# Global attention of a sandwich layer: the lead of the row maxima, its side work, and which engine splits the local weights

## The chip, the cores and the metric

The kernel runs on one core of a Trainium2 chip. The metric is the device time of one launch in microseconds (us). The core has five engines that run side by side, each through its own instructions in order: TensorE (PE, with its weight loads PEld), VectorE (DVE), ScalarE (ACT), GpSimd (POOL) and SyncE (SP), which issues the DMAs. [...]

## The reference, cut to what matters

Two sequences of 2048 tokens with 256 channels go through two residual blocks. In the first, a layer norm is followed by a global attention with 16 heads of 16 channels, rotary positions and a softmax over all 2048 keys, then an output projection and a second layer norm:

```python
q = _rope(proj(Wq, bq)); k = _rope(proj(Wk, bk)); v = proj(Wv, bv)
scores = jnp.einsum('bhtd,bhsd->bhts', q, k) / scale
attn = jax.nn.softmax(scores, axis=-1)
out = jnp.einsum('bhts,bhsd->bhtd', attn, v)
...
x = x + _layernorm(_L0_attn_ref(_layernorm(x), ...))
x = x + _layernorm(_L0_ffn_ref(_layernorm(x), ...))
```

The second block is two layers of local attention (8 heads of 64 channels, windows of 128 tokens) with a gated feed-forward network each. The change touches the first block and the passage to the second.

## The kernel before, in words

**Units and steps.** The global attention is cut into 32 units: for each of two batches `b`, four groups `g` of four heads, and four blocks `k` of 512 queries. `attend` (L505) takes a unit in 16 steps, one for each 128 keys: per step four score matrices `se` of 128 keys by 512 queries on PE (L543), an exponential of each on ACT (L548, `pe<-se`), and the products with the values on PE (L517, `pv`, one step later). The first four units (`HALVED`) are done in two halves of eight steps.

**Maxima ahead.** The exponentials need the row maxima first. `row_max` (L437) computes the scores a second time with the queries as rows (`sm`, L412), and DVE reduces each 128 by 512 tile to one column (L452, `pm<-sm`). Four such reductions are one step's worth. When a unit (or half) is complete, `finish_max` (L469) combines the columns on DVE (`nm`, L472), splits the result in two parts on POOL (`mp`, L477 and L478; on DVE for the last unit), and yields. `DELAY` groups of four reductions later the rest follows: a transpose on PE (`tn`, L481), a copy on ACT (`mt`, L485), a DMA to a DRAM tile (`md`, L488) and four DMAs that put the maxima into two extra rows of the unit's queries `qs` (L491), so that the score product subtracts them. The last unit's rest is done by `last_steps` (L895) in its third step.

**The main loop** (L844) runs `len(units) * NT - TAIL` = 486 steps. In step n it draws in turn, so that the engines' orders are written out by hand: three pieces of `attend` and three of the maxima, interleaved; in every fourth step (`EVERY`) two more maxima as long as the lead is below `TAIL` (the maxima start 13 steps ahead and get half a step further each time, up to 26); one piece of the side work that multiplies on PE (`side.step(PRODUCTS)`); the rest of the step; then pieces on other engines of `early` and `side`. Within `with tc.manual_schedule(engines=ENGINES)`, PE, ACT, DVE and POOL take their instructions in the order of the program; SP's order is the framework's.

**Side work.** `early` normalizes the blocks of batch 1 on POOL and builds the rotary tables of the local layers there. `side` projects: queries of blocks 2 and 3 of batch 0 (`project_qk`, L314), then keys, values and queries of the four blocks of batch 1, and later the closing of finished blocks (`close_in_pieces`, L620). `project_qk` has twelve products, in each of two halves followed by a copy on ACT (`raw`, L329) and two multiplications on POOL (`rotation`, L333); at its end `to_dram_steps` adds six POOL instructions (L342 to L350) and two stores. `load_queries` (L398) reads a unit's queries back when `(n + lead + 3) // NT` reaches its number. In step 3, `output_weights` (L805) loads and splits the output projection's weights and computes its bias with two fp32 matmuls, all at once.

**The startup** ends at L768: `merged` takes pieces of several strands in the order of planned times (first blocks, keys, values, queries of blocks 0 and 1, the first maxima); the framework schedules them.

**The tail.** The last `TAIL` = 26 steps of `attend` have no maxima left beside them. They are a strand with a planned period `STEP` of 2.5 us, ending at `LAST` = 20, beside the strands of the local layers, whose first window starts at 0. Steps here work on double tiles: ACT takes 1024 columns at a time. The planned times of the closing of blocks (−46), of what is left of the side work (−50) and of the weights of the first local layer (`WEIGHTS_FROM` = −50) are set beside it. `load_attn_weights` (L957) copies four pieces of 1024 columns to `attnh` (L196) and subtracts them from the raw weights to `attnl` (L197), both on DVE, each placed behind the last reduction of the maxima (`tc.issue_after(reduced[-1])`).

Of the kernel before, what the change touches and what calls it, by code (L numbers as in the profile page):

```python
# [20 lines left out]
P = 128  # L21
# [26 lines left out]
def tile_sandwich(  # L48
# [152 lines left out]
    def in_order(strands):  # L201


        heap = [(t, n, t, g) for n, (t, g) in enumerate(strands)]
        heapq.heapify(heap)
        return heap
# [225 lines left out]
                yield 1.2 * n  # L432


    reduced, unfinished = [], []

    def row_max():  # L437

        due = []
        for u, (b, g, k) in enumerate(units):  # L440
            q, keys = qs[u], ks[g % 2]
            for span in spans(u):
                if (u, span) == (0, spans(0)[0]):
                    continue
                pm = small.tile([P, 4, 4, NBLK], F32, tag="pm", name="pm", bufs=2)
                for t in range(*span):

                    for j, half in [(j, half) for j in (0, 2) for half in (0, 2)]:
                        for kk, i in ((half, 1), (half, 0), (half + 1, 1), (half + 1, 0)):
                            sc = one("sm", "sm")  # L450
                            scores(q, keys, j + i, t, kk, sc)
                            ins = nc.vector.tensor_reduce(  # L452
                                pm[:, t, j + i, kk : kk + 1], sc, AX.X, ALU.max
                            )
                            reduced[:] = [ins.ins]
# [41 lines left out]
    o_raw = {}  # L497
    sums_d = {}

    TAIL, HALVED, DELAY = 26, 4, 4  # L500


    IN_TURN = {1: (0, 1, 2, 3), 2: (0, 2, 1, 3)}
# [196 lines left out]
    def first_block(k):  # L700
        xt = x0[k]
        for t in range(4):
            shift, rstd = stats0[k][t]
            nc.scalar.activation(xt[:, t, :], xt[:, t, :], AF.Identity, bias=shift, scale=rstd)
        tag = ("qs", "o4", "o4", "t4")[k]
        xh = t4("xh", F32R, tag).rearrange("p (c t) -> p c t", c=2)
        xl = t4("xl", F32R, tag).rearrange("p (c t) -> p c t", c=2)
        for c in range(2):
            yield 1.4 + 0.9 * c
            tp = one("tp")  # L710
            for t in range(4):
                nc.tensor.transpose(tp[:, t * P : (t + 1) * P], xt[:, t, c * P : (c + 1) * P], ident)
            yield 2.3 + 0.9 * c
            split(xh[:, c, :], xl[:, c, :], tp)
        parts0[k] = xh, xl, first_cs if k == 0 else rotary(k, "pe" if k < 2 else "t4")

    def first_project(k, s, eng):
        xh, xl, cs = parts0[k]
# [46 lines left out]
    strands.append((14.7, first_project(0, 0, nc.vector)))  # L765
    strands.append((60.0, first_project(1, 0, nc.gpsimd)))

    merged(in_order(strands))  # L768
    for _ in finish_max(0, spans(0)[0], pm0):
        pass  # L770
    maxima = row_max()
    loaded = 2

    lead, EVERY = 13, 4
    for _ in range(4 * (lead - 8)):
        next(maxima)
    load_keys(0, 1)
# [25 lines left out]
                )  # L803

    def output_weights():  # L805
        raw = split_weights("o", wo1, nc.gpsimd, nc.gpsimd.tensor_copy)

        bo = sb.tile([P, C], F32, tag="bo", name="bo")
        bo_raw = t4("bo_raw")[:, :C]
        nc.sync.dma_start(bo_raw, bo1.partition_broadcast(P))  # L810
        bvs = t2("bvs").rearrange("p (c t) -> p c t", c=4)
        for c in range(2):
            nc.vector.tensor_copy(bvs[:, c, :], bqkv[:, 4 + c : 5 + c].to_broadcast([P, P]))
        pb = one("pb", "sm")
        for c in range(2):
            nc.tensor.matmul(pb[:, :C], bvs[:, c, :], raw[:, c, :], start=(c == 0), stop=(c == 1))
        nc.vector.tensor_tensor(bo, bo_raw, pb[:, :C], ALU.add)
        return bo

    steps = attend()  # L820
    bias_o = []
# [22 lines left out]
    def main_loop(lead, loaded):  # L844
        normalized = {}
        early = Pieces(
            *[normalized_block(1, k, normalized) for k in range(NBLK)],
            *[rotary_tables(l) for l in range(DEPTH)],
        )
        side = Pieces(  # L850
            *[project_qk(0, k, 0, *parts0[k]) for k in range(2, NBLK)],
            *[project(1, k, normalized) for k in range(NBLK)],
        )
        for n in range(1, len(units) * NT - TAIL + 1):


            s, m = steps, maxima
            for strand in (s, m, m, s, s, m):
                next(strand, None)
            if n % EVERY == 0 and lead < TAIL:  # L860
                for _ in range(2):
                    next(maxima)
                lead += 0.5
            side.step(PRODUCTS)
            for strand in (s, m, s):
                next(strand, None)
            early.step(OTHER, WAIT)
# [12 lines left out]
            if (n + lead + 3) // NT >= loaded and loaded < len(units):  # L880
                load_queries(loaded)
                loaded += 1
            if n == 3:
                bias_o.append(output_weights())
        assert next(maxima, 0) == 0 and early.kind is None
        return side

# [14 lines left out]
            yield (n + 1) * STEP  # L902

    strands = [(LAST - TAIL * STEP, last_steps())]
    for i, place in enumerate((LAST + CLOSE, LAST + CLOSE - NT * STEP, -46.0)):
        strands.append((place, close_block(B - 1, NBLK - 1 - i, "t4" if i > 0 else "pe")))

    def last_pieces():
# [1 line left out]
            side.step(PRODUCTS, OTHER, WAIT)  # L910
            yield 0.0

    strands.append((-50.0, last_pieces()))

# [3 lines left out]
    def block():  # L918
        return t4("xb", tag="qs").rearrange("p (t c) -> p t c", t=4)


    zero = sb.tile([1, C], F32, tag="zero", name="zero")
    mid_d = {
        (l, b, k): dram.tile([513, C], F32, name=f"mid_{l}_{b}_{k}")
        for l in range(DEPTH)
# [20 lines left out]
    def raw_columns(src, nk, n, step, tag):  # L946

        sv = src.rearrange("(k p) o -> p k o", p=P)
        for o in range(0, n, step):
            m = min(step, n - o)  # L950
            raw = t4("raw", tag=tag)[:, : nk * m].rearrange("p (k o) -> p k o", k=nk)
            nc.sync.dma_start(raw, sv[:, :, o : o + m])
            yield o, m, raw

    weights = {}

    def load_attn_weights(l, pace, tag, copy):  # L957
        tiles = [large_v(0, f"attnh_{l}", F32R), large(0, f"attnl_{l}", F32R)]
        n = 2 * 3 * INNER
        wq = [t[:, :n].rearrange("p (k o) -> p k o", k=2) for t in tiles]  # L960
        wo = [t[:, n : n + 4 * C].rearrange("p (k o) -> p k o", k=4) for t in tiles]
        weights["attn", l] = wq, wo
        if l == 0:
            nc.gpsimd.memset(zero, 0.0)
        t = 0.0

        for n in (1, 0, 2):
            cols = slice(n * INNER, (n + 1) * INNER)
            for _, _, raw in raw_columns(wqkv2[l][:, cols], 2, INNER, INNER, tag):
                yield t + 4.0  # L970
                with tc.issue_after(reduced[-1]):
                    split(wq[0][:, :, cols], wq[1][:, :, cols], raw, copy=copy)
                t += pace
                yield t
        for _, _, raw in raw_columns(wo2[l], 4, C, C, tag):
            yield t + 4.0
            with tc.issue_after(reduced[-1]):
                split(wo[0], wo[1], raw, copy=copy)

    def load_ffn_weights(l, pace):  # L980
        gb = sb.tile([P, 4], F32, tag="gb", name=f"gb_{l}")
# [56 lines left out]
    FFN_PERIOD, FFN_START = 22.2, 25.0  # L1038

    TO_FFN, TO_ATTN = 13.0, -3.0  # L1040
    WEIGHTS_FROM = -50.0
    MANUAL_FROM = 40.0

    PERIOD = 12.4
# [490 lines left out]
    free = [(-math.inf, MANUAL_FROM)]  # L1535
    BEFORE_FFN, AFTER_FFN = 5.0, 5.0
    BEFORE_ATTN, AFTER_ATTN = -15.0, 25.0
    strands.append((WEIGHTS_FROM, load_attn_weights(0, 2.0, "t4", nc.vector.tensor_copy)))
    ffn_weights_from = LAST + 20.0
    for l in range(DEPTH):  # L1540
        strands.append((ffn_weights_from, load_ffn_weights(l, 20.0)))
# [11 lines left out]
        start += B * NT * PERIOD  # L1553
        free.append((start + BEFORE_FFN, start + AFTER_FFN))
        if l + 1 < DEPTH:
            strands.append((start + 55.0, load_attn_weights(l + 1, 20.0, "pe", nc.scalar.copy)))
        start += TO_FFN
        for n in range(B * NBLK):
            strands.append(
# [105 lines left out]
```

## Time and profile before

| what | before |
| --- | --- |
| time, median of 3 runs | 2881.47 us (2878.64 to 2887.03) |
| time of the profiled execution | 2879.28 us |
| its span, first to last instruction | 2877.5 us |
| mean granted TensorE clock | 0.973 |
| main loop: first to last exponential (steps 1 to 486) | 82.1 to 1480.8 us |
| tail: exponentials of the last 26 steps | 1483.7 to 1557.6 us |
| L452, reductions of the maxima on DVE | 2016, 683 ns mean |
| L548, exponentials on ACT | 1996, 614 ns mean |

In a row of the timeline, the first number is the start in us, the second the busy time, then the engine, the line, the operation, what it writes and reads with its shapes, and the count; in brackets stands the engine's idle time just ahead of it and what ended that. In a row of the windows, behind the stretch and its length, stand the busy us and counts of PE, PEld, DVE, ACT and POOL, then the granted clock of TensorE, the share of the DMA engines, and GB/s.

### The profile page before, as it was taken

How to read it: one execution, taken by the hardware profiler on the slowest of the kernel's cores; microseconds unless marked ns; L12 is line 12 of the kernel's file. 1: busy time of each engine (PE TensorE's matmuls, PEld its weight loads, DVE VectorE, ACT ScalarE, POOL GpSimd, SP SyncE). 2: the span in 40 equal slices, each digit the busy share in tenths (PEclk: the TensorE clock that was granted, in tenths of full speed). 3: DMA queues.
4: the chain of work that ended last, by engine and by line, in shares of the span. 5: the costliest groups of instructions: out<-in, count | busy, mean ns of one | idle time of the engine just before them, and what ended most of it. 6: DMA issues, size and time to landing. Idle time of an engine off the chain costs nothing.

```text
span 2877.5 us, 50638 instructions
## 1 busy us (share of the span) xinstructions
PE 2707.5 (94%) x18496; PEld 1627.8 (57%) x18496; DVE 2317.9 (81%) x5006; ACT 1898.2 (66%) x4015; POOL 1288.1 (45%) x1244
## 2 busy tenths in 40 slices
PE   7989999999999999999988899999999899999998
PEld 5545433333333333333334777777788678787787
DVE  6878888889999999999975788887454788887565
ACT  3456677777878777788876576676443667676432
POOL 4253212131121312200036688886455678786465
PEclk8789999999999999999999999999999999999999
DMA  7033211111111111100022110111232111111232
GB/s 218 20 92 112 67 30 43 42 46 53 40 34 51 52 38 47 54 9 17 18 91 84 52 50 31 32 47 44 81 108 59 54 42 39 34 44 41 82 106 71
DMA packets 154721, 163.72 MB, mean 57 GB/s; under 512 B 32716, under 2 KB 117880, under 8 KB 154472
## 3 DMA queue, kind: packets, MB, share of 16 engines
q1 hardware_dynamic: 154472, 160.48, 18.7%
q8 instruction: 147, 2.41, 0.4%
q14 instruction: 102, 0.84, 0.1%
HBM read 98.89 MB, written 49.04 MB: 51 GB/s over the span
## 4 chain that ended last, share of the span: by engine, by line
PE 74%; DVE 11%; ACT 8%; POOL 3%; issue 2%; DMA 2%; SPq 0%; POOLq 0%; DVEq 0%; ACTq 0%
PE pv L517 17%; PE se L543 15%; ACT pe L548 5%; PE sm L412 4%; PE s L1240 4%; PE o L1307 3%; DVE pm L452 3%; PE w L1289 3%; PE p L172 3%; PE p L176 2%; PE p L174 2%; PE pag L172 2%; PE pag L174 2%; PE pag L176 2%; PE t L1214 2%
## 5 line engine op out<-in xcount | busy, mean ns | idle before, releaser
L452 DVE TENSOR_REDUCE pm<-sm 128x1 f32<-128x512 f32 x2016 | 1247.7, 683 | 119.9 <-PE sm L412 92.0
L548 ACT ACTIVATE pe<-se 128x512 f32<-128x512 f32 (+1 forms) x1996 | 1060.3, 614 | 349.1 <-PE sm L412 258.1
L412 PE MATMUL sm<-ks,qs 48*128 48x512 f32 x2048 | 778.0, 462 | 21.9 <-DMA qs<-qd 8.3
L543 PE MATMUL se<-qs,ks 50*128 50x512 f32 (+1 forms) x2304 | 743.1, 421 | 53.4 <-ACT pe L548 49.8
L543 PEld LDWEIGHTS se<-qs,ks 50*128 50x128 f32 x2304 | 361.3, 190 | 619.6 <-ACT pe L548 536.5
L517 PE MATMUL pv<-pe,va 128*32 128x512 f32 (+1 forms) x4608 | 557.3, 566 | 0.0
L412 PEld LDWEIGHTS sm<-ks,qs 48*128 48x128 f32 x2048 | 355.3, 190 | 62.2 <-DVE pm L452 32.2
L1279 POOL TENSOR_TENSOR e<-e,rs 128x1024 f32<-128x1024 f32 (+1 forms) x128 | 254.2, 1986 | 86.6 <-DVE rs L1275 86.6
L1264 ACT ACTIVATE e<-e,mns 128x256 f32<-128x256 f32 (+1 forms) x512 | 253.4, 498 | 15.4 <-DVE mns L1252 11.7
L477 POOL CAST mp<-nm 128x16 fp32r<-128x16 f32 (+1 forms) x35 | 6.9, 198 | 523.7 <-DVE nm L472 268.6
L95 POOL TENSOR_TENSOR rn<-ss,mhalf 128x8 f32<-128x8 f32 x128 | 214.9, 1679 | 10.6
L1166 ACT ACTIVATE sq<-p 128x512 f32<-128x512 f32 x128 | 76.6, 598 | 173.7 <-PE p L176 171.0
L1252 DVE CUSTOM_DVE_ANT_0 e<-s,mask 128x256 f32<-128x256 f32 (+1 forms) x512 | 181.5, 410 | 10.8 <-PE s L1240 9.4
L1189 POOL TENSOR_TENSOR ra<-qk,tab 128x512 f32<-128x512 f32 x128 | 171.8, 1354 | 18.2 <-DVE qk L1181 18.2
L517 PEld LDWEIGHTS pv<-pe,va 128*32 128x32 f32 x4608 | 99.0, 110 | 134.9 <-issue 107.9
L172 PE MATMUL p<-attnh,xTh 128*128 128x512 f32 x384 | 169.1, 440 | 2.9 <-ACT kT L1227 2.5
L1199 DVE TENSOR_TENSOR rb<-qk,tab 128x256 f32<-128x256 f32 x256 | 164.8, 684 | 0.4 <-PE pv L517 0.2
L1296 ACT COPY eT<-w 128x1024 f32<-128x1024 f32 (+1 forms) x128 | 126.0, 984 | 49.9 <-PE w L1289 47.9
L333 POOL TENSOR_TENSOR rotation<-raw,cs 128x512 f32<-128x512 f32 x40 | 50.4, 1282 | 232.7 <-ACT raw L329 232.7
L174 PE MATMUL p<-attnl,xTh 128*128 128x512 f32 x384 | 153.4, 400 | 0.0
L1240 PE MATMUL s<-kT,qT 64*128 64x256 f32 (+1 forms) x1024 | 142.8, 397 | 11.2 <-ACT qT L1224 3.1
L176 PE MATMUL p<-attnh,xTl 128*128 128x512 f32 x384 | 153.2, 399 | 0.0
(201 smaller groups left out, 4864.4 us busy)
## 6 DMA issues: line engine op xcount, KB each, us to landing
xb<-mid SPq DMA_DIRECT2D x32, 512.0 KB
qs<-qd SPq DMA_DIRECT2D x192, 64.0 KB
kd<-parts SPq DMA_DIRECT2D x16, 512.0 KB
ks<-kd SPq DMA_DIRECT2D x64, 128.0 KB
qd<-parts SPq DMA_DIRECT2D x16, 512.0 KB
tab<-rotary SPq DMA_DIRECT2D x64, 128.0 KB
mid<-xb SPq DMA_DIRECT2D x16, 512.0 KB
xt<-in_x SPq DMA_DIRECT2D x12, 512.0 KB
```

What stands on the lines that cost most here:

```text
L95: nc.gpsimd.tensor_tensor(dst, src, mhalf[:, :n], ALU.pow)
L172: nc.tensor.matmul(out, lh, rh, start=first, stop=False)
L174: nc.tensor.matmul(out, lh, rl, start=False, stop=False)
L176: nc.tensor.matmul(out, ll, rh, start=False, stop=last)
L412: return nc.tensor.matmul(out, q[rows, j // 2, t * P : (t + 1) * P], keys[rows, k, j // 2, :], start=True, stop=True)
L452: ins = nc.vector.tensor_reduce(pm[:, t, j + i, kk : kk + 1], sc, AX.X, ALU.max)
L517: nc.tensor.matmul(pv[SL * j : SL * (j + 1), :w], va[b][:, o : o + SL], pe[c // 1024][:, c % 1024 : c % 1024 + w], start=(s + i == 0), sto ...
L543: nc.tensor.matmul(sc[:, o - c : o - c + w], keys[rows, i // 4, j // 2, i % 4 * P : (i % 4 + 1) * P], q[rows, j // 2, span[0] * P : span[1 ...
L548: nc.scalar.activation(pe[c // 1024][:, c % 1024 : c % 1024 + 512 * m], sc, AF.Exp, scale=1.0 / math.sqrt(D1),)
L1240: nc.tensor.matmul(get(f"s{hf}", two)[:, o + lo : o + 2 * P], at["qT"][own, a * P : (a + 1) * P], kT[own, windows, a, :], start=True, stop ...
L1264: nc.scalar.activation(e4(h // 4)[:, h % 4, lo:], e4(h // 4)[:, h % 4, lo:], AF.Exp, bias=mns[:, h : h + 1], scale=-1.0, accum_out=rs[:, h ...
L1279: nc.gpsimd.tensor_tensor(e4(hf)[:, :, lo:], e4(hf)[:, :, lo:], rs[:, hs].rearrange("p (a o) -> p a o", o=1).to_broadcast([P, 4, 2 * P - lo]),
```

## The change

The lead of the maxima grows to 22 steps and the tail has 22 (`TAIL`); `DELAY` is 1. While the lead grows, the steps with two more maxima draw no product of the side work; the other steps do, and every eighth step (`TWICE`) draws two. The queries of block 2 are projected at the end of the startup (`third_queries`, planned time 101). `output_weights` becomes a generator in `early`, its copies on POOL. The weights of the first local layer are split on POOL, a piece at every fourth step from step 453 on, in place of DVE in the tail. The planned times of one block's closing and of the rest of the side work move from −46 and −50 to −36 and −40; the zeroing of a small tile moves.

```diff
-    TAIL, HALVED, DELAY = 26, 4, 4
+    TAIL, HALVED, DELAY = 22, 4, 1
...
-        parts0[k] = xh, xl, first_cs if k == 0 else rotary(k, "pe" if k < 2 else "t4")
+        parts0[k] = xh, xl, first_cs if k == 0 else rotary(k, "pe" if k < 3 else "t4")
...
+    def third_queries():
+        n = 0.0
+        for kind in project_qk(0, 2, 0, *parts0[2]):
+            if kind == OTHER:
+                n += 1.0
+                yield n
+
+    strands.append((101.0, third_queries()))
     merged(in_order(strands))
...
-    lead, EVERY = 13, 4
+    lead, EVERY, TWICE = 13, 4, 8
...
     def output_weights():
-        raw = split_weights("o", wo1, nc.gpsimd, nc.gpsimd.tensor_copy)
+        t = t4("raw")
+        raw, bo_raw = t[:, :512].rearrange("p (k o) -> p k o", k=2), t[:, 512:768]
+        bvs = t[:, 768:].rearrange("p (c t) -> p c t", c=2)
+        nc.sync.dma_start(bo_raw, bo1.partition_broadcast(P))
+        nc.sync.dma_start(raw, wo1.rearrange("(k p) o -> p k o", p=P))
+        for _ in range(4):
+            yield WAIT
...
+        split(*parts, raw, nc.gpsimd, nc.gpsimd.tensor_copy)
...
         for c in range(2):
-            nc.vector.tensor_copy(bvs[:, c, :], bqkv[:, 4 + c : 5 + c].to_broadcast([P, P]))
+            nc.gpsimd.tensor_copy(bvs[:, c, :], bqkv[:, 4 + c : 5 + c].to_broadcast([P, P]))
+        for _ in range(3):
+            yield WAIT
         pb = one("pb", "sm")
         for c in range(2):
             nc.tensor.matmul(pb[:, :C], bvs[:, c, :], raw[:, c, :], start=(c == 0), stop=(c == 1))
+        yield OTHER
         nc.vector.tensor_tensor(bo, bo_raw, pb[:, :C], ALU.add)
-        return bo
+        bias_o.append(bo)
...
-    def load_attn_weights(l, pace, tag, copy):
+    def load_attn_weights(l, pace, tag, eng, copy):
...
-                with tc.issue_after(reduced[-1]):
-                    split(wq[0][:, :, cols], wq[1][:, :, cols], raw, copy=copy)
+                split(wq[0][:, :, cols], wq[1][:, :, cols], raw, eng, copy)
...
+    def in_steps(generator, waits):
+        for _ in generator:
+            for _ in range(waits):
+                yield WAIT
...
         early = Pieces(
             *[normalized_block(1, k, normalized) for k in range(NBLK)],
+            output_weights(),
             *[rotary_tables(l) for l in range(DEPTH)],
         )
         side = Pieces(
-            *[project_qk(0, k, 0, *parts0[k]) for k in range(2, NBLK)],
+            project_qk(0, 3, 0, *parts0[3]),
             *[project(1, k, normalized) for k in range(NBLK)],
         )
...
             if n % EVERY == 0 and lead < TAIL:
                 for _ in range(2):
                     next(maxima)
                 lead += 0.5
-            side.step(PRODUCTS)
+            else:
+                side.step(PRODUCTS)
+                if n % TWICE == 1:
+                    side.step(PRODUCTS)
...
-            if n == 3:
-                bias_o.append(output_weights())
+
+            if n == (len(units) - NBLK) * NT + 4:
+                early.add(
+                    in_steps(load_attn_weights(0, 0.0, "t4", nc.gpsimd, nc.gpsimd.tensor_copy), 2)
+                )
...
-    for i, place in enumerate((LAST + CLOSE, LAST + CLOSE - NT * STEP, -46.0)):
+    for i, place in enumerate((LAST + CLOSE, LAST + CLOSE - NT * STEP, -36.0)):
...
-    strands.append((-50.0, last_pieces()))
+    strands.append((-40.0, last_pieces()))
...
-    strands.append((WEIGHTS_FROM, load_attn_weights(0, 2.0, "t4", nc.vector.tensor_copy)))
```

More of the change, by code (lines that the diff above doesn't have):

```diff
@@ L432, in first_max @@
                 yield 1.2 * n
-    reduced, unfinished = [], []
+    unfinished = []
     def row_max():
@@ L451, in row_max @@
                             scores(q, keys, j + i, t, kk, sc)
-                            ins = nc.vector.tensor_reduce(
+                            nc.vector.tensor_reduce(
                                 pm[:, t, j + i, kk : kk + 1], sc, AX.X, ALU.max
                             )
-                            reduced[:] = [ins.ins]
                             if (kk, i) != (half + 1, 0):
@@ L805, in output_weights @@
     def output_weights():
-        raw = split_weights("o", wo1, nc.gpsimd, nc.gpsimd.tensor_copy)
+        t = t4("raw")
[5 more added lines that the diff above has]
+            yield WAIT
+        parts = []
+        for s in "hl":
+            t = sb.tile([P, 512], F32R, tag="t2", name=f"o{s}", bufs=10)
+            parts.append(t.rearrange("p (k o) -> p k o", k=2))
+        split(*parts, raw, nc.gpsimd, nc.gpsimd.tensor_copy)
+        w1parts["o"] = parts
         bo = sb.tile([P, C], F32, tag="bo", name="bo")
-        bo_raw = t4("bo_raw")[:, :C]
-        nc.sync.dma_start(bo_raw, bo1.partition_broadcast(P))
-        bvs = t2("bvs").rearrange("p (c t) -> p c t", c=4)
         for c in range(2):
-            nc.vector.tensor_copy(bvs[:, c, :], bqkv[:, 4 + c : 5 + c].to_broadcast([P, P]))
+            nc.gpsimd.tensor_copy(bvs[:, c, :], bqkv[:, 4 + c : 5 + c].to_broadcast([P, P]))
+        for _ in range(3):
+            yield WAIT
         pb = one("pb", "sm")
@@ L816, in output_weights, with raw_columns @@
             nc.tensor.matmul(pb[:, :C], bvs[:, c, :], raw[:, c, :], start=(c == 0), stop=(c == 1))
+        yield OTHER
         nc.vector.tensor_tensor(bo, bo_raw, pb[:, :C], ALU.add)
-        return bo
+        bias_o.append(bo)
+    def raw_columns(src, nk, n, step, tag):
+        sv = src.rearrange("(k p) o -> p k o", p=P)
+        for o in range(0, n, step):
+            m = min(step, n - o)
+            raw = t4("raw", tag=tag)[:, : nk * m].rearrange("p (k o) -> p k o", k=nk)
+            nc.sync.dma_start(raw, sv[:, :, o : o + m])
+            yield o, m, raw
+    weights = {}
+    def load_attn_weights(l, pace, tag, eng, copy):
+        tiles = [large_v(0, f"attnh_{l}", F32R), large(0, f"attnl_{l}", F32R)]
+        n = 2 * 3 * INNER
+        wq = [t[:, :n].rearrange("p (k o) -> p k o", k=2) for t in tiles]
+        wo = [t[:, n : n + 4 * C].rearrange("p (k o) -> p k o", k=4) for t in tiles]
+        weights["attn", l] = wq, wo
+        t = 0.0
+        for n in (1, 0, 2):
+            cols = slice(n * INNER, (n + 1) * INNER)
+            for _, _, raw in raw_columns(wqkv2[l][:, cols], 2, INNER, INNER, tag):
+                yield t + 4.0
+                split(wq[0][:, :, cols], wq[1][:, :, cols], raw, eng, copy)
+                t += pace
+                yield t
+        for _, _, raw in raw_columns(wo2[l], 4, C, C, tag):
+            yield t + 4.0
+            split(wo[0], wo[1], raw, eng, copy)
+    def in_steps(generator, waits):
+        for _ in generator:
+            for _ in range(waits):
+                yield WAIT
     steps = attend()
@@ L922, in tile_sandwich @@
     zero = sb.tile([1, C], F32, tag="zero", name="zero")
+    nc.gpsimd.memset(zero, 0.0)
     mid_d = {
@@ L944, in tile_sandwich @@
     )
[L946 to L955, printed above, removed]
-    def load_attn_weights(l, pace, tag, copy):
[L958 to L970, printed above, removed]
-                with tc.issue_after(reduced[-1]):
-                    split(wq[0][:, :, cols], wq[1][:, :, cols], raw, copy=copy)
[L973 to L978, printed above, removed]
     def load_ffn_weights(l, pace):
@@ L1040, in tile_sandwich @@
     TO_FFN, TO_ATTN = 13.0, -3.0
-    WEIGHTS_FROM = -50.0
     MANUAL_FROM = 40.0
@@ L1555, in tile_sandwich @@
         if l + 1 < DEPTH:
-            strands.append((start + 55.0, load_attn_weights(l + 1, 20.0, "pe", nc.scalar.copy)))
+            strands.append((start + 55.0, load_attn_weights(l + 1, 20.0, "pe", nc.vector, nc.scalar.copy)))
         start += TO_FFN
```

## The prediction, as put on record

> **What bounds the kernel now.** I read the page's busy times first, then the windows of the global attention, then its timeline. A step's start is that of its first of four L548 activations; counting them by fours gives every step's length.
>
> ```profile
> PE 2707.5 (94%) x18496; PEld 1627.8 (57%) x18496; DVE 2317.9 (81%) x5006; ACT 1898.2 (66%) x4015; POOL 1288.1 (45%) x1244
> ...
> 1340.00:1380.00 40.00, 36.97 (x247) 13.00 (x247) 38.16 (x63) 32.12 (x64) 0.42 (x2) 1.00 0.05 11
> ```
>
> The second line is a stretch of steady steps: PE 92% busy, DVE 95%, POOL idle. Such a step takes 2.60 us; with a product of the side work 2.8 us; with two extra maxima as well 4.2 us. No engine has room, so a stall of PE is lost time. PE's idle rows show what exceeds these lengths:
>
> ```profile
> 155.41 0.99 PE L412 MATMUL sm<-ks,qs 48*128 48x512 f32 x2 [5.48 <-DMA qs<-qd]
> 206.16 1.19 PE L412 MATMUL sm<-ks,qs 48*128 48x512 f32 x3 [2.84 <-DMA qs<-qd]
> 320.58 0.47 PE L543 MATMUL se<-qs,ks 50*128 50x512 f32 x1 [2.22 <-DMA qs<-md]
> ...
> 156.00:160.00 4.00, 4.00 (x27) 1.91 (x24) 2.58 (x4) 1.68 (x3) 0.00 (x0) 0.50 0.48 133
> 216.00:220.00 4.00, 4.00 (x29) 2.23 (x26) 2.58 (x4) 2.18 (x5) 0.00 (x0) 0.50 0.07 17
> 328.00:332.00 4.00, 4.00 (x17) 1.16 (x9) 2.10 (x4) 2.01 (x4) 0.00 (x0) 0.50 0.10 25
> ```
>
> Three waits, and behind each the granted clock (third number from the end) is 0.50. By the windows of 4 us it stays there for 6.4, 20.5 and 13.6 us after PE went on. The steps show the whole price: step 18 took 11.1 us for 2.8, so **8.3**; steps 32 to 35 took 8.5, 4.9, 4.9 and 5.2 for 4.2, 2.8, 2.8 and 2.8, so **10.9**; steps 64 to 67 took 6.4, 4.5, 4.9 and 4.9 for 4.2 and three times 2.8, less 0.4 regained: **7.7**. Price less gap, over the time at half clock, is 2.8/6.4, 8.1/20.5 and 5.5/13.6: about 0.40 us lost for each us at half clock.
>
> At the loop's end:
>
> ```profile
> 1481.32 4.65 DVE L196 CAST attnh<-raw 128x1024 fp32r<-128x1024 f32 x4
> 1486.02 4.97 DVE L197 TENSOR_TENSOR attnl<-raw,attnh 128x1024 fp32r<-128x1024 f32 x4
> 1491.50 0.39 PE L481 MATMUL tn<-ident,mp 128*32 128x128 f32 x1 [2.39 <-DVE mp L478]
> ```
>
> DVE splits the local weights before it has the last maxima's parts ready, and PE waits for these.
>
> **The change, part by part**, against the profiled execution (2879.28 us, span 2877.5; the median shown is 2.2 higher).
>
> *Third queries ahead, Q of block 2 in the startup.* Block 3 is then first in the side work: its 12 products end at step 17, not 25, and its load is issued at step 29. Both waits for qs<-qd go: −8.3 −10.9. What is added in the startup is 12 products of 512 columns, 0.43 us each at the 0.5 clock that holds from 56 to 104: up to 5.2 us. DVE reduces without a pause from 57 to 76 and 78 to 95, and PE is the slack one there, so from −4 (an earlier full clock) to +5.2; I take +2, DVE being the nearer row. POOL is idle there; SP has two more stores.
>
> *Maxima passed on one step later instead of four.* Unit 4's maxima reach qs three steps earlier, some 8.5 us against a wait of 2.2: −7.7. What it uncovers is below.
>
> *Output weights in pieces.* Step 3 took 6.9 us for 2.8 (DVE copies, two fp32 matmuls, a store behind them). The copies go to an idle POOL; matmuls and addition come back later at about 1.7: −2.4.
>
> *Lead 22, and pairs of maxima in steps of their own.* 18 pairs instead of 26: 8 × 1.4 = −11.2. The loop gets four more steady steps: 4 × 2.60 = +10.4. Side products leave the paired steps and come twice in one step of eight; 0.2 to 0.4 each wherever they are, so 0 by the same count.
>
> *Tail of 22.* Undisturbed tail steps take 2.03 us (activations at 1497.7 to 1504.7): 4 × 2.03 = −8.1. Its last maxima are now needed four steps (8.1 us) after `tn`, and took 6.7 (1491.5 to the issue's end plus a landing) before: 0 to +4, taken +1.
>
> *Local weights on POOL.* The tail's first two steps took 9.0 us (1483.7 to 1492.7) for 4.1: −4.9. On POOL, by its rows of 512 elements (0.61 cast, 1.28 subtraction), a piece of 1024 is 3.8 us, four of them in steps 455 to 467, where POOL is idle and none stands ahead of maxima (458, 474): 0. [...]
>
> Gains 53.5, costs 13.4: 2879.3 − 40.1 = **2839**, if the shorter delay costs nothing.
>
> **What the delay hid.** `finish_max` puts `nm` on DVE, `mp` on POOL, and `DELAY` groups later `tn` on PE; all three run in program order. In steady steps `tn` started 8.7 us after `nm` ended; three steps less leave 0.9 (1.2 to 1.3 where products fill PE). `mp` ends 0.64 us after `nm` when POOL is free: just in time. But POOL isn't always free:
>
> ```profile
> 391.94 2.52 POOL L333 TENSOR_TENSOR rotation<-raw,cs 128x512 f32<-128x512 f32 x2 [16.60 <-ACT raw L329]
> 394.55 1.29 POOL L342 TENSOR_TENSOR rotation<-rotation 128x512 f32<-128x512 f32 x1
> 395.90 0.61 POOL L348 CAST parts<-rotation 128x512 fp32r<-128x512 f32 x1
> 396.59 1.31 POOL L350 TENSOR_TENSOR parts<-rotation,parts 128x512 fp32r<-128x512 f32 x1
> 397.85 1.27 POOL L345 TENSOR_TENSOR rotation<-rotation 128x512 f32<-128x512 f32 x1
> 399.19 0.61 POOL L348 CAST parts<-rotation 128x512 fp32r<-128x512 f32 x1
> 399.88 1.28 POOL L350 TENSOR_TENSOR parts<-rotation,parts 128x512 fp32r<-128x512 f32 x1
> 401.60 0.20 POOL L477 CAST mp<-nm 128x16 fp32r<-128x16 f32 x1 [0.44 <-DVE nm L472]
> ```
>
> The end of a projection holds POOL for 9.3 us, and the maxima queue behind it. Here they came three steps later and met it by 0.4 us. Where do they stand after the change? Reductions done by step n are 52 + 4n + 2 per pair: unit u (from 4 on) ends at step 16u − 6 (was 16u − 10). Counting the yields of the side work (before: bursts in 85, 109, 127, as the trace has them) puts them in 37, 105 and 121, the last normalization of a closing block in 377, a closing block's multiplication in 473. Maxima end in 39, 106, 122, 378, 474: **five times one or two steps behind a burst.** From burst start S: `mp` done at S+9.85; `nm` in the next step S+2.7, `tn` wanted at S+4.0, so PE waits 5.8 us, twice. In step 39: 9.85 − 5.8 = 4.0. In 378 (1206.04 to 1212.35 before): 4.4. In 474 (1445.77 to 1452.4): 5.0. That is 25.0; in the last two DVE has some 1.5 us of reductions queued: **22.0**. The bounds are 0 (nothing meets) and 25.
>
> Then the clock. All gaps are longer than 2.22 us, which halved it. Time at half clock after PE went on: 6.4, 20.5, 13.6, and 4.9 in the tail (1491.5 to 1496.4), mean 11.3; × 0.40 × 5 = **22.6**, bounds 10 (4.9) and 41 (20.5). [...]
>
> 2839.2 + 22.0 + 22.6 = **2884**.
>
> **Rivals.**
> *The waits are met* (faster, about 2848; 2838 to 2866): the bursts fall a step off my count, or PE finds the parts made. For it: 32 of 36 finishes had `mp` within 0.65 us of `nm`. Against: the count fits every burst of before, and lags of 2.7, 3.1 and 3.0 us are there already (the fourth is the last unit's, on DVE). With none met 2839; with two of five, 2857.
> *The clock stays down* (slower, about 2902): each of the five stalls, at steps 39, 106, 122, 378 and 474, is followed by 20.5 us at half clock, as at 206 us: 2839.2 + 22 + 41. It decides from about 9 us each: there stalls and clock eat the 40. For it: the sample nearest in work had 20.5 and the next 13.6.
> *It doesn't do what it says:* unit 4's parts still come late because SP has ks<-kd loads ahead of them, which wait on PE (up to 9.3 us): +7.7 on any case; in the chances it is within the others.
>
> **Chances.** The likeliest case, five stalls with a mean aftermath (2872 to 2897): 0.52, of it 0.05 faster, 0.30 the same, 0.17 slower. Waits met: 0.32, all faster. Clock down: 0.16, all slower. What a measurement can tell is 0.3%, 8.6 us around the median of 2881.5. So faster 0.37, the same 0.30, slower 0.33. Range 2846 to 2906: from the first rival's lower half to the second's upper.
>
> **What would show it.** Right: step 18 at 2.8 us and no PE wait for qs<-qd; step 65 without a gap; `tn` waiting for POOL `mp` L478 five times for 4 to 6 us, with clock 0.50 behind; tail steps of 2 us from the first on, DVE without attnh. Wrong: `tn` never waiting over 1 us (then 2839); a startup later than before by 5 us; a tail that doesn't shorten by 13; the clock at 1.00 through a wait of 5 us.

## The result, and the profile after

The changed kernel is **slower**: median 2912.98 us of 4 executions (2901.53 to 2924.34) against 2884.25 (2878.64 to 2887.96) for the kernel before on the same chip, ratio 1.0101, 95% interval 1.0054 to 1.0149. The forecast was 2884, the range ended at 2906. The profiled execution took 2907.78 us, its span is 2905.1 (27.6 more) and its mean granted clock 0.963 (0.973 before).

By the page of the changed kernel the engines did almost the same work as before:

```profile
PE 2721.0 (94%) x18496; PEld 1639.0 (56%) x18496; DVE 2308.3 (79%) x4996; ACT 1899.1 (65%) x4023; POOL 1295.1 (45%) x1254
```

DVE has ten instructions and 9.6 us less and POOL ten instructions more (weights and copies), PE has the same 18496 instructions but 13.5 us more busy time, which fits its lower mean clock. Where the 27.6 us arose, by the starts of the exponentials:

| stretch | before | after | difference |
| --- | --- | --- | --- |
| startup, to the first step | 82.1 | 86.1 | +4.0 |
| steps 1 to 128 | 436.8 | 431.9 | −4.9 |
| steps 129 to 480 | 945.0 | 964.1 | +19.1 |
| step 481 to the first tail step | 19.8 | 34.4 | +14.6 (four more steps: 10.4) |
| tail | 73.9 | 66.2 | −7.7 (four fewer steps) |
| after the tail | 1319.9 | 1322.4 | +2.5 |

What was to go is gone: there is no wait for qs<-qd, step 18 takes 2.8 us, step 65 has no gap. In its place come five waits. These are all the rows of PE in the changed kernel's timeline where `tn` waited over 1 us for the parts on POOL; the number in the bracket is the wait. (Most lines of the first part stand one lower in the changed kernel, L480 for the L481 of before.)

```profile
231.93 0.38 PE L480 MATMUL tn<-ident,mp 128*16 128x128 f32 x1 [4.29 <-POOL mp L477]
445.99 0.40 PE L480 MATMUL tn<-ident,mp 128*32 128x128 f32 x1 [5.43 <-POOL mp L477]
498.79 0.40 PE L480 MATMUL tn<-ident,mp 128*32 128x128 f32 x1 [5.43 <-POOL mp L477]
1201.30 0.40 PE L480 MATMUL tn<-ident,mp 128*32 128x128 f32 x1 [3.98 <-POOL mp L477]
1461.47 0.40 PE L480 MATMUL tn<-ident,mp 128*32 128x128 f32 x1 [4.70 <-POOL mp L477]
```

They stand where the prediction counted them, one step behind its finishes in 39, 106, 122, 378 and 474: by the starts of the exponentials they end in steps 40, 107, 123, 379 and 475. They last 23.83 us together; 25.0 was counted and 22.0 charged. The second one, with the burst (the run of POOL instructions that ends a projection) from the queue of POOL, and `nm` from DVE:

```profile
436.36 2.52 POOL L333 TENSOR_TENSOR rotation<-raw,cs 128x512 f32<-128x512 f32 x2 [11.32 <-ACT raw L329]
...
439.17 0.22 DVE L471 TENSOR_REDUCE nm<-pm 128x16 f32<-128x64 f32 x1
...
444.23 1.26 POOL L350 TENSOR_TENSOR parts<-rotation,parts 128x512 fp32r<-128x512 f32 x1
445.44 0.20 POOL L476 CAST mp<-nm 128x16 fp32r<-128x16 f32 x1
445.71 0.22 POOL L477 TENSOR_TENSOR mp<-nm,mp 128x16 fp32r<-128x16 f32 x1
```

`nm` ends at 439.39, 3 us into the burst; 0.4 us of work on `mp` begins at 445.44, when the burst is through, and its end at 445.93 releases `tn` at 445.99. The windows around it (behind the lengths: busy us of PE, PEld, DVE, ACT and POOL, then the clock):

```profile
440.00:444.00 4.00, 0.56 (x3) 0.24 (x2) 1.81 (x4) 1.35 (x3) 3.79 (x5) 0.79 0.20 77
444.00:448.00 4.00, 2.01 (x9) 0.30 (x9) 0.00 (x0) 0.73 (x2) 2.48 (x6) 0.50 0.51 189
448.00:452.00 4.00, 4.00 (x22) 1.61 (x18) 2.58 (x4) 2.17 (x4) 1.17 (x1) 0.50 0.23 54
```

While PE waits, DVE runs dry as well (0.00 in the second row), so the time is lost for both; then PE goes on at half clock until 452.5. The stretches at half clock over the five waits last 20.5, 10.2, 10.2, 17.1 and 13.7 us.

Two more waits of PE were in no step of the prediction. ACT casts `oh` for a closing block, and the exponentials queue behind that cast:

```profile
1501.52 0.62 ACT L594 CAST oh<-rb 128x512 fp32r<-128x512 f32 x1 [2.93 <-POOL rb L592]
1502.69 0.49 PE L542 MATMUL se<-qs,ks 50*128 50x512 f32 x1 [3.12 <-ACT pe L547]
...
1547.13 0.62 ACT L594 CAST oh<-rb 128x512 fp32r<-128x512 f32 x1 [4.29 <-POOL rb L592]
1548.72 1.71 PE L542 MATMUL se<-qs,ks 50*128 50x512 f32 x4 [3.76 <-ACT pe L547]
```

In each pair the first row is the cast, waiting for POOL's multiplication (whose own waits, of 8.70 and 3.66 us, are for the DMA rb<-rsum), and the second is PE, out of exponentials. One lies in the loop's end, which the shorter tail has made longer, the other in the tail: 6.88 us, with 10.2 and 6.8 us at half clock. The kernel before had such a wait too, at the start of its tail:

```profile
1483.18 0.62 ACT L595 CAST oh<-rb 128x512 fp32r<-128x512 f32 x1 [2.41 <-POOL rb L593]
1484.78 0.50 PE L543 MATMUL se<-qs,ks 50*128 50x512 f32 x2 [1.59 <-ACT pe L548]
```

And there is half clock with no wait over 0.7 us ahead of it, as at 131.7 to 148.8:

```profile
128.00:132.00 4.00, 3.56 (x34) 2.03 (x30) 3.79 (x8) 2.21 (x5) 0.00 (x0) 0.96 0.02 4
132.00:136.00 4.00, 4.00 (x25) 2.35 (x17) 3.14 (x7) 1.57 (x3) 0.00 (x0) 0.50 0.01 4
```

One of the executions of the experiments, the profiled one of delay3, was disturbed (6347 us); it is left out everywhere, and the trace of delay3_oh_pool is read in its place.

### The profile page after: what moved, and what is told of

It reads as the page before. It is cut to its first block, busy times and chain, and to the rows that moved or that the text cites. A ratio compares the mean times of both kernels' runs of the same rounds, so it can differ in the third digit from the quotient of the medians.

```text
span 2905.1 us, 50624 instructions
## 1 busy us (share of the span) xinstructions
PE 2721.0 (94%) x18496; PEld 1639.0 (56%) x18496; DVE 2308.3 (79%) x4996; ACT 1899.1 (65%) x4023; POOL 1295.1 (45%) x1254
## 3 DMA queue, kind: packets, MB, share of 16 engines
q8 instruction: 146, 2.39, 0.3%
## 4 chain that ended last, share of the span: by engine, by line
PE 73%; DVE 11%; ACT 8%; POOL 4%; issue 3%; DMA 1%; SPq 1%; POOLq 0%; DVEq 0%; ACTq 0%
PE pv L516 16%; PE se L542 15%; ACT pe L547 5%; PE sm L412 5%; DVE pm L452 4%; PE s L1267 4%; PE o L1334 3%; PE w L1316 3%; PE p L172 3%; PE p L174 2%; PE p L176 2%; PE pag L172 2%; PE pag L174 2%; PE pag L176 2%; PE t L1241 2%
## 5 line engine op out<-in xcount | busy, mean ns | idle before, releaser
L542 PE MATMUL se<-qs,ks 50*128 50x512 f32 (+1 forms) x2304 | 752.8, 426 | 57.5 <-ACT pe L547 56.9
L542 PEld LDWEIGHTS se<-qs,ks 50*128 50x128 f32 x2304 | 369.9, 194 | 636.9 <-ACT pe L547 538.0
L516 PE MATMUL pv<-pe,va 128*32 128x512 f32 (+1 forms) x4608 | 567.3, 575 | 0.0
L1291 ACT ACTIVATE e<-e,mns 128x256 f32<-128x256 f32 (+1 forms) x512 | 252.9, 497 | 15.2 <-DVE mns L1279 11.6
L95 POOL TENSOR_TENSOR rn<-ss,mhalf 128x8 f32<-128x8 f32 x128 | 214.7, 1678 | 10.6
```

The source lines that it names most:

```text
L95: nc.gpsimd.tensor_tensor(dst, src, mhalf[:, :n], ALU.pow)
L516: nc.tensor.matmul(pv[SL * j : SL * (j + 1), :w], va[b][:, o : o + SL], pe[c // 1024][:, c % 1024 : c % 1024 + w], start=(s + i == 0), sto ...
L542: nc.tensor.matmul(sc[:, o - c : o - c + w], keys[rows, i // 4, j // 2, i % 4 * P : (i % 4 + 1) * P], q[rows, j // 2, span[0] * P : span[1 ...
L1291: nc.scalar.activation(e4(h // 4)[:, h % 4, lo:], e4(h // 4)[:, h % 4, lo:], AF.Exp, bias=mns[:, h : h + 1], scale=-1.0, accum_out=rs[:, h ...
```

## How the clock is separated from the work

Executions of one kernel differ: those of the kernel before spanned 2864.3 to 2903.5 us. The granted clock is 1.0 or 0.5 in the records, so an execution's mean clock c and its span give its time at half clock, 2 × (1 − c) × span. Over all 150 executions of the two kernels and of those below, the span is a constant of the kernel plus 0.385 (±0.018) us for each us at half clock; what is left has a root mean square of 2.1 us. The prediction had read 0.40 from three stalls. So each kernel has two numbers: its **constant** (the span it would have at full clock throughout; differences hold to ±2 to 4 us) and its mean **half-clock time**, whose difference counts 0.385 each. The second scatters more: executions of one kernel differ by 21 us (root mean square), so a mean of 4 holds to about ±20 us and one of 10 to ±13, which is ±8 and ±5 us of time.

| kernel | executions | constant | half-clock time |
| --- | --- | --- | --- |
| before | 62 | 2816.9 | 168 |
| after | 4 | 2822.6 | 229 |
| delay3 | 3 | 2801.2 | 133 |
| oh_pool | 10 | 2816.2 | 197 |
| delay3_oh_pool | 4 | 2794.6 | 144 |
| parts_dve | 4 | 2822.1 | 244 |
| before_third | 10 | 2811.7 | 152 |
| before_weights_pool | 10 | 2814.2 | 160 |
| before_delay1 | 10 | 2818.0 | 174 |
| best_pairs_products | 10 | 2808.7 | 180 |
| best_delay2 | 7 | 2806.0 | 174 |
| best_lead26 | 10 | 2806.0 | 174 |
| best_weights_dve | 6 | 2801.1 | 153 |

From before to after the constant grows by 5.7 us, and 61 us more at half clock cost 23.3 (±8): most of the loss is clock.

## The experiments

Theory A: the shorter delay costs the change its gain, by five waits for `mp` behind bursts of POOL and the half clock behind them, and the closing blocks' cast adds to it. The rivals: that it is the clock or the steps without products, whatever the delay; that the other parts gain less than was counted.

**The delay alone undone** (delay3):

```diff
-    TAIL, HALVED, DELAY = 22, 4, 1
+    TAIL, HALVED, DELAY = 22, 4, 3
```

> The changed kernel with a delay of three groups instead of one, nothing else. Theory A (five waits of PE at tn for POOL's mp, 23.8 us together in the profile, and the half clock behind them, some 50 us by the lengths of the steps around them): tn waits nowhere more than 0.7 us, the clock stays at 1.00 there, and the time falls by 40 to 50 us, to 2863 to 2873 us. Rival B (with a lead of 22 the maxima then come too late for their unit): PE waits at the first score product of many units for the maxima's DMA, 1 to 4 us each, and the time stays above 2895 us.

2856.12 us, ratio to before 0.9914 (0.9883 to 0.9945). That is 57 us less than after, and the sign of the change turns. By the table it is 21.4 (±3.7) of constant, against waits of 23.83 in the profile, and 96 us less at half clock, 36.8 (±12). That is more than the 40 to 50 expected. Theory A holds for most of the loss; that no `tn` waits for `mp` with this delay is seen in the trace of delay3_oh_pool below.

**The parts on DVE, delay as in the change** (parts_dve):

```diff
-        eng = nc.gpsimd if u < len(units) - 1 else nc.vector
+        eng = nc.vector
```

> The changed kernel with the maxima's two parts (mp) made on DVE for every unit, as before only for the last. Theory A (POOL's queue is what tn waits for): no wait of PE at tn above 0.7 us; DVE, 95% busy, gets 34 times 0.5 us, so the time falls by about 50 and rises by about 17, to about 2880 us. Rival C (what was lost lies elsewhere, and the waits only took the place of others): 2913 plus 17, about 2930 us.

2919.9 us, 1.0138 (1.0085 to 1.019). The number that theory A gave is missed. No `tn` waits for `mp` any more, but the constant is as after's (−0.5 ± 3.0). The 70 instructions that moved are not small for DVE: its busy time on the page is 2325.5 against 2308.3, 17.2 us more, on the engine that was 95% busy in a steady step. So 23.8 us of waits went and 17.2 us of work came to an engine with no room, and in the loop PE now waits for DVE six times, 0.8 to 2.7 us each, 9.0 us together. That these two make up the whole 23.8 is not shown. One of the six, and the windows around it:

```profile
291.65 0.37 PE L480 MATMUL tn<-ident,mp 128*32 128x128 f32 x1 [1.08 <-DVE pm L452]
```

```profile
288.00:292.00 4.00, 2.92 (x27) 1.45 (x26) 3.90 (x8) 1.77 (x4) 4.00 (x6) 0.96 0.94 272
302.00:322.00 20.00, 20.00 (x103) 9.10 (x102) 11.42 (x18) 9.64 (x18) 0.69 (x1) 0.50 0.17 47
```

Behind a wait of 1.08 us the clock stayed down for 51.2 us. The experiment says that the waits can be moved, not that they cost nothing; it does not tell A from its rivals, delay3 does.

**The cast on POOL** (oh_pool):

```diff
-            nc.scalar.copy(oh[:, c, :], rb[:, c, :])
+            nc.gpsimd.tensor_copy(oh[:, c, :], rb[:, c, :])
```

> The changed kernel with the upper halves oh of a closing block in the tail copied on POOL, not on ACT. Theory D (ACT, in order, waits for POOL's rb behind a DMA, once within the main loop and once in the tail, with PE gaps of 3.1 and 3.8 us and the half clock behind the first): both gaps go, 8 to 12 us less, about 2903 us. Rival: POOL's copy comes as late and another wait takes their place: 2908 to 2918 us.

2894.55 us, 1.0041 (1.0017 to 1.0065), 18 less than after: 6.4 (±2.6) of constant, where the two waits had been 3.12 and 3.76 us, and 12.0 (±9) of clock. The waits behind the cast are gone from the trace, the five for `mp` are there as before. The 17.1 us at half clock behind the two waits would be 6.6 us of that clock; with the 6.9 us of the waits this makes 13.5, a little over the 8 to 12 expected. The rest of the 18 is within the scatter.

**Both** (delay3_oh_pool: the two edits together):

> The changed kernel with a delay of three groups and, in the tail's closing blocks, oh copied on POOL instead of ACT. The delay alone gave 2856 us, the copies alone took 18 us off the changed kernel. If these are two causes that add (theory A for the waits at tn, theory D for ACT's wait behind POOL and a DMA), the time is 2838 us, which is also what the prediction gave for a change whose shorter delay costs nothing (2839). If the copies only gained by moving clock phases, it stays at 2850 to 2856.

2849.35 us, 0.9895 (0.9866 to 0.9925): the best version, ahead of both kernels, but 11 us above the 2838 of two causes that add. In the constants they add: it falls by 6.7 (±3.3) from delay3, again the two waits, and by 21.6 (±2.7) from oh_pool, again the five. In the clock they do not: from delay3 the half-clock time does not fall, from oh_pool it falls by 20.5 (±9) us of time, where delay3 had 36.8 (±12) from after. The bursts are still there, and `mp` is still late, behind the same instructions:

```profile
436.71 1.28 POOL L350 TENSOR_TENSOR parts<-rotation,parts 128x512 fp32r<-128x512 f32 x1
437.95 0.19 POOL L476 CAST mp<-nm 128x16 fp32r<-128x16 f32 x1
438.22 0.22 POOL L477 TENSOR_TENSOR mp<-nm,mp 128x16 fp32r<-128x16 f32 x1
```

`nm` had ended at 431.79, so the parts are 6.66 us late, as late as in the changed kernel (6.5). But `tn` comes at 439.21 in the program's order and does not wait for `mp`. In the five finishes behind a burst the lag is 5.65, 6.66, 6.68, 4.22 and 5.78 us, and `tn` comes 5.5 to 8.3 us behind `nm`: the delay hides the burst, it does not remove it.

**Two steps** (best_delay2: delay3_oh_pool with `DELAY` 2):

> The changed kernel with the maxima passed on two steps later and with the closing blocks' cast on GpSimd; its neighbour with three steps has a median of 2849.35. In the neighbour's trace the parts of the maxima are done 5.65, 6.66, 6.68, 4.22 and 5.78 us after nm in the five steps behind a burst, and PE asked for them 6 to 7 us after nm. One step less puts the asking at some 3.5 to 4 us, so PE waits five times for 0.4 to 2.8 us, some 9 us in all. Theory A (what counts is the wait, and a wait of 1.5 us or more also halves the clock): 9 us and about four aftermaths of 10 us at 0.40, so 2866 to 2876. Rival (short waits cost only themselves): 2856 to 2860. Rival (delay as such costs or saves nothing once the cast is moved): 2849.

2877.71 us, 0.9949 (0.99 to 0.9997), from 2853.91 to 2895.96. The constant is 11.5 (±2.7) above its neighbour's; the five waits in the trace are 2.06, 2.14, 2.73, 1.35 and 2.30, together 10.6. The median is just above theory A's range (2866 to 2876). Single executions scatter over those of both rivals, but the constant carries the five waits, so the rival without a loss is out. Of the clock it shows something new. The two extremes differ by 42 us, and their half-clock times are 220 and 125 us, the latter less than the mean of the neighbour without waits (144). So waits of about 2 us seem to halve the clock in some executions and not in others; only the slowest one has a trace. In that one:

```profile
500.72 0.28 PE L480 MATMUL tn<-ident,mp 128*32 128x128 f32 x1 [2.73 <-POOL mp L477]
1204.88 0.28 PE L480 MATMUL tn<-ident,mp 128*32 128x128 f32 x1 [1.35 <-POOL mp L477]
```

Behind the first the records have 20.5 us at half clock, behind the second 3.4. The 1.5 us that theory A named for halving was the author's estimate, and no run shows it as a limit: here half clock followed a wait of 1.35 us.

**The delay alone made, on the kernel before** (before_delay1: `DELAY` 4 to 1):

> The kernel before with a delay of one group instead of four, nothing else. Theory A: in its order only three finishes of the maxima stand close behind a burst on POOL (lags of 2.7, 3.1 and 3.0 us in its profile), so tn waits three times for 1.4 to 2.1 us, each with 4 to 5 us of half clock behind it, against 7.7 us gained at unit 4: 2884 to 2895 us. Rival E (a delay of one is bad in itself, at every finish): tn waits over 0.7 us at many of the 35 finishes and the time is above 2905 us.

2888.8 us, 1.0018 (0.9988 to 1.0047), as A expected. `tn` waits for `mp` behind a burst at 255.02 (1.75 us) and 1177.23 (2.33), twice where three were expected: at the third place PE itself is late, waiting 5.88 us for qs<-qd. Unit 4's wait is gone. Elsewhere the bursts of the kernel before miss the maxima. So the delay by itself is not dear. It is dear together with the other parts, which shift the side work against the maxima.

**Third queries alone, on the kernel before** (before_third: the hunks `k < 3`, `third_queries` and `project_qk(0, 3, ...)` of the change):

> The kernel before with the queries of block 2 projected in the startup, nothing else. As predicted: both PE waits for the queries (5.5 and 2.8 us) and the half clock behind them go, 19 us, against 2 to 4 us more in the startup: about 2868 us against 2884. Rival: the startup or another wait takes it back: 2880 to 2888 us.

2870.76 us, 0.9966 (0.9946 to 0.9987): constant −5.2 (±1.5), clock −6.4. Both waits for qs<-qd (8.32 us) are gone; unit 4's wait, which the longer delay still has, grew from 2.22 to 3.88 us, and the loop starts at 85.2 and not at 82.1.

**Local weights on POOL alone, on the kernel before** (before_weights_pool: `load_attn_weights` with POOL's copies and subtractions, in `early`, as in the change):

> The kernel before with the weights of the first local layer split on POOL within the main loop, nothing else. As predicted: DVE is free at the start of the tail, PE's waits there (1.6, 1.2 and 2.4 us) go, 5 us less, and with the half clock behind them up to 9: 2875 to 2879 us. Rival: ACT's wait for POOL at the same place remains the later one, or moves into the loop: 2882 us or more.

2877.43 us, 0.9985 (0.9963 to 1.0006): as expected, but the ratio's interval reaches 1; constant −2.7 (±1.5). Of PE's three waits at the start of the tail only the last, 2.39 us for DVE, is gone. The two behind ACT's cast remain (1.21 and 0.93 us), as the rival had it:

```profile
1479.89 0.50 PE L543 MATMUL se<-qs,ks 50*128 50x512 f32 x2 [1.21 <-ACT pe L548]
```

**The same edit undone in the best version** (best_weights_dve):

```diff
-            if n == (len(units) - NBLK) * NT + 4:
-                early.add(
-                    in_steps(load_attn_weights(0, 0.0, "t4", nc.gpsimd, nc.gpsimd.tensor_copy), 2)
-                )
...
+    strands.append((-50.0, load_attn_weights(0, 2.0, "t4", nc.vector, nc.vector.tensor_copy)))
```

> The same neighbour (2849.35) with the local weights split by VectorE in the tail, as the kernel before does, and not by GpSimd in the loop. By the prediction's term it loses 4.9 us: 2854. Theory A: 2852 to 2857, the tail's first steps long and DVE attnh in them. Rival (the GpSimd pieces take as much from the loop's last steps as VectorE takes from the tail): 2848 to 2851.

2861.85 us, 0.9908 (0.9879 to 0.9937), 12.5 above its neighbour's median: constant +6.5 (±2.8), clock 3.3. The time is above the 2852 to 2857 expected; the constant agrees with the 4.9 that was counted. Here the cast is on POOL, so ACT's wait does not stand beside DVE's.

**A lead of 26 in the best version** (best_lead26: `TAIL` 26):

> The same neighbour (three steps, cast on GpSimd, 2849.35) with a lead of 26 steps in place of 22: eight pairs of maxima more in steps of their own, four tail steps more, four loop steps fewer. By the terms of the prediction (8 x 1.4 + 4 x 2.03 - 4 x 2.60) it is 8.9 us slower, 2858. Theory A: 2855 to 2861. Rival (the shorter lead gave nothing, its gain went into closing work that the shorter tail no longer covers): 2846 to 2851.

2876.46 us, 0.9967 (0.994 to 0.9993), 27 above its neighbour and 15 above the upper end expected: constant +11.4 (±2.6), clock +11.6 (±9). The constant is close to the 8.9 of the prediction's terms and two new waits:

```profile
899.46 0.28 PE L480 MATMUL tn<-ident,mp 128*32 128x128 f32 x1 [0.98 <-POOL mp L477]
1075.04 0.28 PE L480 MATMUL tn<-ident,mp 128*32 128x128 f32 x1 [2.28 <-POOL mp L477]
```

With this lead the bursts stand elsewhere, the parts lag by 7.1 and 7.8 us, and three steps no longer cover them.

**Products in every step** (best_pairs_products: delay3_oh_pool with the products as before the change):

```diff
-            else:
-                side.step(PRODUCTS)
-                if n % TWICE == 1:
-                    side.step(PRODUCTS)
+            side.step(PRODUCTS)
```

> The kernel with a delay of three and oh on POOL, but with products of the side work in every step, as before the change, also in those with two more maxima, and never two in one step. If taking the products out of the paired steps is what let the clock fall without a wait (17 and 7 us at half clock near steps 12 and 28 of the changed kernel), this one has clock 1.00 there and gains 5 to 10 us over its neighbour of this call; if the product's place is neutral, as predicted, both are within 5 us.

2881.29 us, 0.9988 (0.9969 to 1.0007), 32 us above its neighbour, where a gain of 5 to 10, or at most 5 either way, was expected. Both expectations are wrong: the clock is low near the same steps with products in every step (10.2 us at 129.3, 17.1 at 160.0), and the products' place is not neutral. The constant is 14.2 (±2.6) higher, the clock costs 14.0 (±9) more. PE's waits of over 1 us within the loop are 1.62 us for `mp` at 212.87, 1.84 for a qs<-md at 1120.32, and one for unit 4's queries. SP's queue ahead of that one, and the wait on PE:

```profile
308.50 7.70 SPq L392 DMA_DIRECT2D ks<-kd  x8
316.32 1.01 SPq L808 DMA_DIRECT2D rotary<-tab  x2
317.42 3.40 SPq L392 DMA_DIRECT2D ks<-kd  x4
320.91 0.37 SPq L487 DMA_DIRECT2D md<-mt  x1
```

```profile
325.28 0.76 PE L542 MATMUL se<-qs,ks 50*128 50x512 f32 x1 [5.95 <-DMA qs<-md]
```

`mt` was ready at 312.79; its store was issued 8.1 us later, behind loads of keys. That is the prediction's third rival, in another kernel: the path by SP decides unit 4, and where the side work stands decides what SP has ahead. The three waits make 9.4 of the 14.2 us of constant; the rest of it is not settled.

## Right and wrong, by the prediction's steps

**The waits were right.** Five were foreseen, in these steps, from a count of yields and one burst's rows; they last 23.83 us against 25.0, and the delay alone is worth 21.4 of constant against the 22.0 charged.

**The step that failed: a wait of ACT that was put at nothing.** The prediction looked for what queues behind a wait on POOL and on PE, not on ACT. Its terms for the tail took undisturbed steps (−8.1) and put the whole 4.9 us at the tail's start down to DVE's weights. The trace of before has ACT waiting 2.41 us there for POOL, with the cast of `oh`, and PE behind it; with the weights on POOL alone PE's waits behind it remained (1.21 and 0.93 us for 1.59 and 1.17). In the changed kernel the cast holds up the exponentials twice, 6.88 us of PE's time. That one line on POOL takes 18 us off the changed kernel, 6.4 of constant and 12.0 (±9) of clock, and its 2894.55 us lies inside the range that the change itself overshot. With the longer delay it is worth 6.8 us. The tail, with one of the two waits in it, became 7.7 and not 12 us shorter. Which of the moved parts (lead, tail, planned times) put the cast where it now stands was not separated.

**The clock behind the five waits was not clearly mis-sized.** The term is "mean 11.3; × 0.40 × 5 = 22.6", that is 56.5 us at half clock after PE went on. In the profile of the changed kernel it is 61.6 us (19.2, 6.6, 8.4, 15.8 and 11.7), in that of oh_pool, with the same five waits, 35.4. By the fit the delay is worth 36.8 (±12) us of clock with the cast on ACT and 20.5 (±9) with it on POOL, one above the term and one below. The price of a us was right (0.385).

**Half clock elsewhere was missed.** By the prediction's figures 40 us at half clock were to go and 56.5 to come, +16; the difference between the two kernels is +61 (±21). In the profile 17.1 us stand behind the casts, and 23.9 at 131.7 and 189.7, with no wait over 0.7 us ahead of them. The prediction had no term for either; why the clock falls without a wait stays open.

**The gains were nearly right in work, less so in clock.** The sum without the shorter delay's costs was −40.1, of which the prediction's own figures put 16.4 down to clock (price less gap, 2.8, 8.1 and 5.5) and so 23.7 to work. Delay3 gives −29 against before (−15.6 constant, −13.5 clock). Delay3_oh_pool, which also has the cast on POOL, gives −22.3 (±2.3) of constant and −9.3 (±8) of clock: 2849, where 2839 was forecast. The waits for qs<-qd and unit 4's went; the lead was worth 8.1 of constant (11.4 less the two new waits) for 8.9; the weights 6.5 for 4.9 in the best version. The products' place, put at 0, was not: with products in every step the best version lost 32 us. The startup took 4.0 us longer for the 2 taken, inside the bounds of −4 and 5.2.

**One reading was off.** In the example of a burst the maxima did not meet it: the 0.44 us in the bracket is POOL standing idle until `nm` came. The count of the five waits did not rest on it.

**The range was too narrow** because its cases held the five stalls and their clock, and nothing else that could be late. The rival with 2902 came near by luck: it had 20.5 us at half clock behind each stall, the profile has 12.3 on average. What lifts the result beyond it is the cast, and half clock elsewhere.

## What to carry to other kernels

A delay in the program's order between a producer and its consumer is cover for the longest burst of the engine in between: before it is shortened, compare it with that burst's length, not with the usual lag (6.7 against 0.64 us here), and for every instruction that moves, look at what queues behind it on its own engine. Do the same for waits that the trace already has: before one is put down to a single engine, look at which engine's wait ends last once that one is free. Price a stall as the wait plus what each us at half clock costs (0.385 us here, by the fit), and leave room in the range for half clock that no wait explains. When executions of one kernel differ by more than the effect sought, fit the span against the granted clock first, and compare the constants.

## What the runs showed of the clock

In the traces of before and after, all 66 changes of the clock lie, within a trace, on a fixed grid of 3.413 us, to 0.03 us. From 20 to 1640 us I took each window of that grid at full clock and the share of it in which PE was busy. Busy less than half: 14 of 14 were followed by half clock. 50 to 80%: 3 of 16. 80 to 90%: 3 of 134. Above 90%: none of 701. It does not hold from the start on: in the first 20 us, 9 windows busy less than half were followed by full clock.

By the waits: in the same stretch and traces, all 14 waits of PE of 2.22 us or more that began at full clock were followed by half clock, among them the five of 3.98 to 5.43 us at `tn`. Of the five of 1.34 to 1.41 us, two were. The waits of the trace of best_delay2, 1.35 to 2.73 us, lie between; that their place on the grid made the spread of its executions is the author's estimate, not shown. The half clock with no wait over 0.7 us, in the changed kernel's loop behind windows busy 87 and 83% (from 128.3 and 186.3), remains unexplained; it is in delay3_oh_pool too (13.7 us at 130.0, 17.1 at 304.1), and products in every step did not remove it.

One full window is often not enough for the way back: of 65 windows at half clock in which PE was busy over 97%, in the same stretch and traces, 20 were followed by full clock. What decides it stays open.
